# Finding a capacity threshold two bits per step instead of one, in a post-LN mixture-of-experts block on one Trainium2 core

## The chip, the cores and the metric

The program runs on one core of one Trainium2 chip. The metric is device time in microseconds (us) of one execution; the value for a kernel is the median of several executions, and lower is better. A separate execution is recorded by the hardware profiler and gives the profile and the trace that are read below.

## The reference, cut to what matters

The block has two layers, each an attention-like mixer and a mixture of experts, with layer normalisation after each. The change is in the first mixture of experts, where every expert chooses its tokens:

```python
T = B * S                      # 8 * 512 = 4096 tokens
cap = max(1, T // E)           # E = 8 experts, so 512 tokens each
probs = jax.nn.softmax(xt @ Wg, axis=-1)
pT = probs.T                   # 8 x 4096
_, top_idx = jax.lax.top_k(pT, cap)
sel = zeros((E, T), bool).at[arange(E)[:, None], top_idx].set(True)
masked = where(sel, pT, -inf)
assigned = sel.any(axis=0)
tok2exp = where(assigned, argmax(masked, axis=0), argmax(pT, axis=0))
```

So each expert needs its 512 largest probabilities out of 4096. The kernel gets them through a threshold: for each expert, the largest 32-bit pattern t such that at least 512 of its probabilities, read as floats, are at or above t. Probabilities lie between 0 and 1, and for non-negative floats the order of the bit patterns is the order of the values, so t can be found bit by bit from the top, from bit 29 down to bit 0.

## The kernel before, in words

The program has four stages, one after the other: three recurrent layers (`recurrent_layers`), the first mixture of experts (`expert_choice_layer`), attention (`attention_layer`), and the second mixture of experts (`token_choice_layer`). In the profiled execution the recurrent layers end at about 402 us, and the expert stage's first dense matmuls start after 500 us.

Between these lies the routing. `expert_choice_gates` (L1009) computes the softmax over eight experts (L1020 to L1031), transposes it on TensorE into `pt`, copied to SBUF at L1040, in which 16 partitions hold one expert, each with 256 of its tokens, and then searches the threshold in a loop of 30 steps over bits 29 to 0:

- L1055, VectorE: compare all 128 x 256 probabilities with the candidate `cand` and add up the hits of each partition into `cnt` (one instruction with an accumulator output; the profile shows it as two, TENSOR_SCALAR_CACHE_REDUCE and DVE_READ_ACCUMULATOR).
- L1059, TensorE: multiply by the matrix `blk` of ones in 16 x 16 blocks, so that every partition of an expert gets that expert's total `tot`, in PSUM.
- L1061, VectorE: `less` = (tot < 512) times the bit.
- L1063, VectorE: one instruction that clears the bit where there were too few and sets the next bit to be tried.

Each step needs the step before, so the loop is one chain that goes from VectorE to TensorE and back. After it, L1075 to L1114 turn the threshold into the choice `M` of an expert for each token, L1137 to L1160 into places in the experts' lists, and L787 to L820 into a table of tiles. GpSimd then writes the tokens into the lists (L731), SyncE loads the expert weights that the table names (L925), and the expert matmuls follow.

The order within the engines around the loop is set by a scheduler, which fills each engine's queue in program order as far as data and buffers allow; the stages before and the list writing after have their order written out by hand. Two queues matter besides VectorE and TensorE. GpSimd fills a tile `m0none` (memset L723) and writes numbers into it (iota L724). SyncE then issues small loads and stores in this order: L710, L713, L715, then L727, which stores `m0none` and waits for the iota, then L1014, which loads `blk`, and L1016. The first matmul of the search needs `blk`.

Of the kernel before, what the change touches and what calls it, by code (L numbers as in the profile page):

```python
# [10 lines left out]
F32 = mybir.dt.float32  # L11
I32 = mybir.dt.int32
AF = mybir.ActivationFunctionType
ALU = mybir.AluOpType
# [3 lines left out]
P = 128  # L18
# [8 lines left out]
CAP = T // E0  # L27
# [981 lines left out]
def expert_choice_gates(nc, rp, psR, ident, lg, a, M, W):  # L1009


    NS = NC // 2
    blk = rp.tile([P, P], F32, name="blk")
    nc.sync.dma_start(blk, a["c_blk"])  # L1014
    low = rp.tile([P, P], F32, name="low")
    nc.sync.dma_start(low, a["c_low"])  # L1016

    ex = rp.tile([P, NC, E0], F32, name="ex0")
    st = rp.tile([P, NC], F32, name="st0")
    nc.vector.reduce_max(st, lg, AX.X)  # L1020
    nc.vector.tensor_sub(ex, lg, st.unsqueeze(2).to_broadcast([P, NC, E0]))
    nc.scalar.activation(ex, ex, AF.Exp)
    nc.vector.reduce_sum(st, ex, AX.X)
    nc.vector.reciprocal(st, st)
    pr = rp.tile([P, 2, E0, NS], F32, name="pr0")
    for jh in range(2):
        nc.vector.tensor_mul(
            pr[:, jh].rearrange("p e s -> p s e"),
            ex.rearrange("p (s j) e -> p j s e", j=2)[:, jh],
            st.rearrange("p (s j) -> p j s", j=2)[:, jh].unsqueeze(2).to_broadcast([P, NS, E0]),  # L1030
        )  # L1031


    pt_ps = psR.tile([P, 2 * P], F32, tag="x", name="pt_ps")
    for jh in range(2):
        nc.tensor.transpose(
            pt_ps[:, jh * P : (jh + 1) * P], pr[:, jh].rearrange("p e s -> p (e s)"), ident
        )
    pt = rp.tile([P, 2 * P], F32, name="pt")
    nc.vector.tensor_copy(pt, pt_ps)  # L1040

    one = rp.tile([P, 1], F32, name="one")
    nc.vector.memset(one, 1.0)
    desc = rp.tile([P, E0, NS], F32, name="desc")
    for e in range(E0):
        nc.vector.memset(desc[:, e, :], float(E0 - e))

    cand = rp.tile([P, 1], I32, tag="cand", bufs=2, name="cand29")  # L1050
    nc.vector.memset(cand, 1 << 29)
    for bit in range(29, -1, -1):
        hit = rp.tile([P, 2 * P], F32, tag="hit", bufs=2, name=f"hit{bit}")
        cnt = rp.tile([P, 1], F32, tag="cnt", bufs=2, name=f"cnt{bit}")
        nc.vector.tensor_scalar(  # L1055
            hit, pt, cand.bitcast(F32), None, ALU.is_ge, ALU.add, accum_out=cnt
        )
        tot = psR.tile([P, 1], F32, tag="x", name=f"tot{bit}")
        nc.tensor.matmul(tot, blk, cnt, start=True, stop=True)  # L1059
        less = rp.tile([P, 1], I32, tag="less", bufs=2, name=f"less{bit}")  # L1060
        nc.vector.tensor_scalar(less, tot, float(CAP), float(1 << bit), ALU.is_lt, ALU.mult)  # L1061
        new = rp.tile([P, 1], I32, tag="cand", bufs=2, name=f"cand{bit - 1}")
        nc.vector.scalar_tensor_tensor(  # L1063
            new, less, (1 << bit) >> 1, cand, ALU.bitwise_or, ALU.bitwise_xor
        )
        cand = new
    thr = cand

    thr_f = thr.bitcast(F32)
    sel = rp.tile([P, 2 * P], F32, name="sel")  # L1070
    eq = rp.tile([P, 2 * P], F32, name="eq")
    rank = rp.tile([P, 2 * P], F32, name="rank")
    ngt = rp.tile([P, 1], F32, name="ngt")
    left = rp.tile([P, 1], F32, name="left")
    nc.vector.tensor_scalar(sel, pt, thr_f, None, ALU.is_gt, ALU.add, accum_out=ngt)  # L1075

    sl_ps = psR.tile([P, 2, 4 * P], F32, tag="s", bufs=1, name="sl_ps")[:, :, :P]
    S = sl_ps.rearrange("p j (e s) -> p j e s", e=E0)
    for jh in range(2):
        nc.tensor.matmul(  # L1080
            sl_ps[:, jh, :], sel[:, jh * P : (jh + 1) * P], ident, start=True, stop=False
        )
    nc.vector.tensor_scalar(eq, pt, thr_f, None, ALU.is_equal)
    nc.vector.tensor_tensor_scan(
        rank, one.to_broadcast([P, 2 * P]), eq, 0.0, ALU.mult, ALU.add
    )
    before = psR.tile([P, 1], F32, tag="x", name="before")
    nc.tensor.matmul(before, blk, ngt, start=True, stop=False)
    nc.tensor.matmul(before, low, rank[:, 2 * P - 1 : 2 * P], start=False, stop=True)
    nc.vector.tensor_scalar(left, before, -1.0, float(CAP), ALU.mult, ALU.add)  # L1090
    nc.vector.scalar_tensor_tensor(eq, rank, left, eq, ALU.is_le, ALU.mult)
    for jh in range(2):
        nc.tensor.matmul(
            sl_ps[:, jh, :], eq[:, jh * P : (jh + 1) * P], ident, start=False, stop=True
        )


    def across(src, dst):
        nc.vector.tensor_reduce(dst, src.rearrange("p j e s -> p j s e"), AX.X, ALU.max)

    def spread(v):
        return v.unsqueeze(2).to_broadcast([P, 2, E0, NS])

    sl = rp.tile([P, 2, E0, NS], F32, name="sl")
    top = rp.tile([P, 2, NS], F32, tag="top", bufs=2, name="top0")
    across(S, top)
    nc.vector.tensor_sub(sl, spread(top), S)
    nc.vector.scalar_tensor_tensor(pr, sl, -4.0, pr, ALU.mult, ALU.add)
    across(pr, W)
    nc.vector.tensor_tensor(sl, pr, spread(W), ALU.is_equal)  # L1110
    nc.vector.tensor_mul(sl, sl, desc.unsqueeze(1).to_broadcast([P, 2, E0, NS]))
    top = rp.tile([P, 2, NS], F32, tag="top", bufs=2, name="top1")
    across(sl, top)
    nc.vector.tensor_tensor(  # L1114
        M.rearrange("p (s j) e -> p j e s", j=2), sl, spread(top), ALU.is_equal
    )


def expert_choice_layer(tc, pre, x_ext, lg, ident, rows, a):
# [3 lines left out]
    with ExitStack() as ctx:  # L1123
# [6 lines left out]
        nc.vector.memset(keep, 1.0)  # L1130
        nc.vector.memset(keep[:, :, 0:1], 0.0)
        expert_choice_gates(
            nc, rp, psX, ident, lg, a, M, x_ext[:, :, D].rearrange("p (s j) -> p j s", j=2)
        )
# [824 lines left out]
```

## Time and profile before

| what | value |
|---|---|
| median of 7 executions | 1996.2 us (1989.55 to 1999.2) |
| profiled execution, its own time | 1998.94 us |
| span in its trace, first to last instruction | 1997.1 us |
| mean granted TensorE clock over the span | 0.930 |
| TensorE matmul busy | 1737.8 us (87%) |
| VectorE busy | 1132.4 us (57%) |
| ScalarE busy | 1002.3 us (50%) |
| GpSimd busy | 523.1 us (26%) |
| threshold search, first L1055 to first L1075 | 406.32 to 453.04 us: 46.72 us |

In the profile, PE is TensorE (PEld its weight loads), DVE is VectorE, ACT is ScalarE, POOL is GpSimd and SP is SyncE (SPq its queue of transfers). Times on the trace are us from the start of the span. A line of the timeline gives start, duration, engine, source line, operation, output tile and input tiles, the shape, the count, and in brackets how long the engine had been idle and what released it. The float32 matmul of the search appears as two matmul records and two weight loads.

### The profile page before, as it was taken

Reading aid. Unit: us, or ns where it says so; the run is one execution under the profiler, and the core shown is the slowest. Engines: PE = TensorE matmul, PEld = TensorE weight load, DVE = VectorE, ACT = ScalarE, POOL = GpSimd, SP = SyncE. Lnnn points to the kernel's source line nnn. Section 1 sums busy time; section 2 is a strip of 40 time slices with the busy share of each in tenths; the row PEclk is TensorE's granted clock in tenths of the full one; section 3 lists DMA queues with packets and bytes.
Section 4 is the critical chain, followed back from the end, with each engine's and each line's share of the span. In section 5 each row is a group of like instructions: output and inputs, shape, how many; then the busy total and the mean of one; then the engine's idle time right before and its main releaser. Section 6 shows DMA issues by size and latency. Waiting matters only on the chain.

```text
span 1997.1 us, 31137 instructions
## 1 busy us (share of the span) xinstructions
PE 1737.8 (87%) x10398; PEld 1136.3 (57%) x10398; DVE 1132.4 (57%) x2844; ACT 1002.3 (50%) x2166; POOL 523.1 (26%) x447
## 2 busy tenths in 40 slices
PE   6999995531799698898989998987999999999995
PEld 2555553321699584222222222323889999999994
DVE  6999998853122531676777786884534222222226
ACT  5899976500132321457666767655534334333343
POOL 1000000004422221001041423233666644444440
PEclk9999998655899797899999999998999999999998
DMA  9990000004554300000010211122675667566548
GB/s 358 402 386 1 1 0 1 32 7 171 187 176 147 118 1 20 13 17 17 17 58 16 62 32 42 46 76 74 175 203 127 152 159 184 110 145 140 117 103 255
DMA packets 115262, 217.10 MB, mean 109 GB/s; under 512 B 17101, under 2 KB 85919, under 8 KB 108320
## 3 DMA queue, kind: packets, MB, share of 16 engines
q1 hardware_dynamic: 81536, 165.77, 25.1%
q0 software_dynamic: 30560, 46.72, 11.5%
q10 hardware_dynamic: 3008, 2.63, 0.4%
q8 instruction: 84, 1.38, 0.3%
q14 instruction: 74, 0.61, 0.1%
HBM read 244.79 MB, written 100.43 MB: 173 GB/s over the span
## 4 chain that ended last, share of the span: by engine, by line
PE 54%; issue 7%; DVE 6%; DMA 4%; ACT 4%; POOL 4%; SPq 0%; POOLq 0%; another core or an unknown queue 0%; ACTq 0%; DVEq 0%
PE s L1668 13%; PE m1h L956 12%; PE m1o L978 12%; PE po L1704 5%; PE qk L1640 3%; PE bv L1587 2%; DVE nmx L1758 2%; ACT pe L1765 2%; DMA res<-z,m0xg 2%; PE v L1566 1%; PE m1xp L943 1%; POOL res L1205 1%; PE t L1680 1%; POOL m0rows L731 1%; PE tot L1059 1%
## 5 line engine op out<-in xcount | busy, mean ns | idle before, releaser
L1758 DVE TENSOR_REDUCE nmx<-s 128x1 f32<-128x512 f32 x512 | 330.0, 686 | 161.6 <-PE t L1680 103.3
L1765 ACT ACTIVATE pe<-t 128x512 f32<-128x512 f32 x512 | 277.8, 594 | 210.2 <-PE t L1680 198.5
L1668 PE MATMUL s<-kT,qT 32*128 32x512 f32 x1024 | 304.5, 669 | 54.5 <-ACT pe L1765 25.7
L1680 PE MATMUL t<-qA,kT 32*128 32x512 f32 x1024 | 293.2, 649 | 2.5 <-ACT pe L1765 2.0
L1817 POOL DMA_INDIRECT acc<-y,at x143 | 221.6, 1550 | 256.7 <-DVE at L1810 161.5
L1668 PEld LDWEIGHTS s<-kT,qT 32*128 32x128 f32 x1024 | 81.8, 190 | 221.6 <-ACT pe L1765 174.6
L962 ACT ACTIVATE m1hT<-m1h,m1ws 128x128 f32<-128x128 f32 x284 | 103.4, 367 | 155.5 <-PE m1h L956 129.3
L962 ACT ACTIVATE m1hT<-m1h,xT 128x128 f32<-128x128 f32 x288 | 105.4, 368 | 149.5 <-PE m1h L956 133.6
L945 DVE COPY m1xq<-m1xp 128x256 f32<-128x256 f32 x143 | 60.6, 424 | 184.6 <-PE m1xp L943 101.6
L1816 DVE TENSOR_SCALAR y<-m1o,gt 128x256 f32<-128x256 f32 x143 | 69.1, 483 | 168.3 <-PE m1o L978 158.3
L731 POOL DMA_INDIRECT m1rows<-x_ext,slot x128 | 126.8, 990 | 120.8 <-ACT pe L1765 77.7
L956 PE MATMUL m1h<-m1xq,xT 128*128 128x128 f32 x1152 | 142.8, 277 | 4.5 <-DVE m1xq L945 3.2
L956 PEld LDWEIGHTS m1h<-m1xq,xT 128*128 128x128 f32 x1152 | 140.8, 194 | 9.2 <-issue 3.6
L956 PEld LDWEIGHTS m1h<-m1xq,m1ws 128*128 128x128 f32 x1136 | 138.7, 193 | 7.0 <-issue 3.5
L956 PE MATMUL m1h<-m1xq,m1ws 128*128 128x128 f32 x1136 | 140.1, 277 | 2.4 <-DVE m1xq L945 2.3
L1704 PE MATMUL po<-pe,V 128*17 128x512 f32 x1024 | 137.4, 609 | 1.2 <-ACT pe L1765 1.2
L978 PE MATMUL m1o<-xT,m1hT 128*128 128x256 f32 x576 | 137.4, 380 | 0.7 <-issue 0.5
L978 PE MATMUL m1o<-m1ws,m1hT 128*128 128x256 f32 x568 | 134.9, 379 | 0.0
L1734 POOL TENSOR_TENSOR AO<-AO,on 128x256 f32<-128x256 f32 x32 | 23.5, 734 | 353.3 <-DVE on L1729 335.7
L964 ACT ACTIVATE m0hT<-m0h 128x128 f32<-128x128 f32 x156 | 43.0, 277 | 143.7 <-PE m0h L956 116.3
L978 PEld LDWEIGHTS m1o<-xT,m1hT 128*128 128x128 f32 x576 | 103.4, 190 | 12.1 <-ACT m1hT L962 0.7
L978 PEld LDWEIGHTS m1o<-m1ws,m1hT 128*128 128x128 f32 x568 | 102.3, 191 | 10.8
(358 smaller groups left out, 2999.5 us busy)
## 6 DMA issues: line engine op xcount, KB each, us to landing
xT<-in_w_pack SPq DMA_DIRECT2D x72, 1034.0 KB
m1ws<-in_w_pack SPq DMA_DIRECT2D x71, 1034.0 KB
m0ws<-in_w_pack SPq DMA_DIRECT2D x39, 1034.0 KB
m0rows<-zero SPq DMA_DIRECT2D x5, 6360.0 KB
m1xg<-m1rows SPq DMA_DIRECT2D x143, 138.0 KB
acc<-zero SPq DMA_DIRECT2D x2, 4096.0 KB
f<-acc SPq DMA_DIRECT2D x16, 512.0 KB
m0rows<-zero SPq DMA_DIRECT2D x1, 4770.0 KB
```

What stands on the lines that cost most here:

```text
L731: ins = self.nc.gpsimd.indirect_dma_start(out=self.rows[:, :], out_offset=bass.IndirectOffsetOnAxis(ap=place, axis=0), in_=row, in_offset= ...
L945: nc.vector.tensor_copy(xq, ps)
L956: nc.tensor.matmul(ps, w[:, o : o + P], xq[:, dc, :], start=(dc == 0), stop=(dc == DC - 1),)
L962: ins = nc.scalar.activation(hT[:, fc, :], ps, AF.Gelu, bias=w[:, o : o + 1])
L978: nc.tensor.matmul(ps, hT[:, fc, :], w[:, o : o + D], start=(fc == 0), stop=(fc == FC - 1))
L1668: mm = nc.tensor.matmul(ps, qTs[u % NR][r, qc * P : (qc + 1) * P], kTs[u % NR][r, :], start=True, stop=True,)
L1680: mm = nc.tensor.matmul(ps, kTs[v % NR][r, kc * P : (kc + 1) * P], qAs[v][r, :], start=True, stop=True,)
L1704: mm = nc.tensor.matmul(po[h4 * HP : h4 * HP + VW, :], V[:, b * NQ + kc, 4 * g + h4, :], pes.pop((u, kc, h4)), start=(kc == 0), stop=(kc = ...
L1758: ins = nc.vector.tensor_reduce(at, ps, AX.X, ALU.max, negate=True)
L1765: ins = nc.scalar.activation(pe, ps, AF.Exp)
L1816: nc.vector.tensor_scalar_mul(y, ps, gt)
L1817: nc.gpsimd.indirect_dma_start(out=R.acc[t % 2][:, :], out_offset=bass.IndirectOffsetOnAxis(ap=at, axis=0), in_=y, in_offset=None, compute ...
```

## The change

The loop takes 15 steps instead of 30. In each, three candidates are counted: the bits found so far with the next two bits set to 01, 10 and 11. The number of candidates with at least 512 hits, 0 to 3, is the value of the two bits. A table `digit` holds, for each step, the four values 0, 1, 2 and 3 times the step's unit; it is filled by 60 memsets of one column each on GpSimd, which in the program stand ahead of the loop. The vector of four candidates for the next step is made by two VectorE instructions: multiply the count by the unit and add the next step's row of `digit`, then or the result with the bits found so far. The last step makes only the result.

```diff
-    cand = rp.tile([P, 1], I32, tag="cand", bufs=2, name="cand29")
-    nc.vector.memset(cand, 1 << 29)
-    for bit in range(29, -1, -1):
-        hit = rp.tile([P, 2 * P], F32, tag="hit", bufs=2, name=f"hit{bit}")
-        cnt = rp.tile([P, 1], F32, tag="cnt", bufs=2, name=f"cnt{bit}")
-        nc.vector.tensor_scalar(
-            hit, pt, cand.bitcast(F32), None, ALU.is_ge, ALU.add, accum_out=cnt
-        )
-        tot = psR.tile([P, 1], F32, tag="x", name=f"tot{bit}")
+    steps = [1 << bit for bit in range(28, -2, -2)]
+    digit = rp.tile([P, len(steps), 4], F32, name="digit")
+    for i, u in enumerate(steps):
+        for j in range(4):
+            nc.gpsimd.memset(digit[:, i, j : j + 1], float(j * u))
+    cand = rp.tile([P, 4], I32, tag="cand", bufs=2, name="cand0")
+    nc.vector.tensor_copy(cand, digit[:, 0, :])
+    for i, u in enumerate(steps):
+        cnt = rp.tile([P, 3], F32, tag="cnt", bufs=2, name=f"cnt{i}")
+        for j in range(3):
+            hit = rp.tile([P, 2 * P], F32, tag="hit", bufs=2, name=f"hit{i}_{j}")
+            nc.vector.tensor_scalar(
+                hit, pt, cand.bitcast(F32)[:, j + 1 : j + 2], None, ALU.is_ge, ALU.add,
+                accum_out=cnt[:, j : j + 1],
+            )
+        tot = psR.tile([P, 3], F32, tag="x", name=f"tot{i}")
         nc.tensor.matmul(tot, blk, cnt, start=True, stop=True)
-        less = rp.tile([P, 1], I32, tag="less", bufs=2, name=f"less{bit}")
-        nc.vector.tensor_scalar(less, tot, float(CAP), float(1 << bit), ALU.is_lt, ALU.mult)
-        new = rp.tile([P, 1], I32, tag="cand", bufs=2, name=f"cand{bit - 1}")
-        nc.vector.scalar_tensor_tensor(
-            new, less, (1 << bit) >> 1, cand, ALU.bitwise_or, ALU.bitwise_xor
-        )
+        k = rp.tile([P, 1], F32, tag="digits", bufs=2, name=f"k{i}")
+        reach = rp.tile([P, 3], F32, tag="reach", bufs=2, name=f"reach{i}")
+        nc.vector.tensor_scalar(reach, tot, float(CAP), None, ALU.is_ge, ALU.add, accum_out=k)
+        more = rp.tile([P, 4], I32, tag="more", bufs=2, name=f"more{i}")
+        new = rp.tile([P, 4], I32, tag="cand", bufs=2, name=f"cand{i + 1}")
+        if i + 1 < len(steps):
+            nc.vector.scalar_tensor_tensor(
+                more, k.to_broadcast([P, 4]), float(u), digit[:, i + 1, :], ALU.mult, ALU.add
+            )
+        else:
+            nc.vector.tensor_scalar_mul(more, k.to_broadcast([P, 4]), float(u))
+        nc.vector.tensor_tensor(new, more, cand[:, 0:1].to_broadcast([P, 4]), ALU.bitwise_or)
         cand = new
+    cand = cand[:, 0:1]
     thr = cand
```

In the built program of the changed kernel, the order of all other instructions on each engine is as before. The 60 memsets stand in GpSimd's queue between the memset L723 and the iota L724; the copy that makes the first candidates stands in VectorE's queue where the memset L1051 stood, ahead of the reciprocal L1024.

## Prediction

> **What bounds the kernel now.** The page's shares over the whole span do not settle this change: TensorE is busy 87% of the time, but the search sits in a stretch where nearly everything else is idle. So I read the chain of work that ended last, cut to the search (406.3 to 453.1 us):
>
> ```profile
> by line: PE tot L1059 38.4%; DVE hit L1055 32.0%; DVE less L1061 10.9%; DVE cand L1063 10.6%; issue 7.7%; DVE sel L1075 1.0%; DVE cand-1_2589 L1063 0.4%
> ```
>
> The whole stretch is one chain through the four instructions of the loop; the table of the same stretch has ScalarE and GpSimd at 0.00 us, transfers at a share of 0.00, and a granted TensorE clock of 0.50. Nothing hides the loop, and it hides nothing. One step, from the timeline (PE weight-load line left out):
>
> ```profile
> 409.49 0.48 DVE L1055 TENSOR_SCALAR_CACHE_REDUCE hit<-pt,cand 128x256 f32<-128x256 f32 x1
> 409.89 0.08 DVE L1055 DVE_READ_ACCUMULATOR hit<-pt,cand 128x1 f32 x1
> ...
> 410.03 0.58 PE L1059 MATMUL tot<-cnt,blk 128*128 128x1 f32 x2 [0.97 <-DVE hit L1055]
> 410.65 0.16 DVE L1061 TENSOR_SCALAR less<-tot 128x1 int32<-128x1 f32 x1 [0.68 <-PE tot L1059]
> 410.85 0.16 DVE L1063 SCALAR_TENSOR_TENSOR cand<-less,cand 128x1 int32<-128x1 int32 x1
> 411.04 0.48 DVE L1055 TENSOR_SCALAR_CACHE_REDUCE hit<-pt,cand 128x256 f32<-128x256 f32 x1
> ```
>
> A step is 411.04 - 409.49 = 1.55 us: 1.16 from the start of the count to the start of `less` (count, trip to TensorE and back), 0.20 for `less`, 0.19 for `cand`. An instruction that waits for its forerunner on VectorE starts 0.04 us after that one's end. Thirty steps take 406.32 to 453.04, 46.72 us.
>
> **What the change removes, adds and moves.** VectorE's main instructions stay at 90 (30 x 3 before, 15 x 6 after). What goes is 15 trips to TensorE; what comes is that three counts stand side by side without data between them, and that the last three instructions of a step are a little longer.
>
> *The three counts.* The first and second need only the candidates. The third reuses the first one's `hit` buffer (two buffers) and so waits for the first count, which ends 0.48 us after its start. How closely counts follow each other when nothing holds them, no row shows for this very form; these come nearest, the start of an instruction behind an accumulating one with no wait in between:
>
> ```profile
> 380.15 0.42 DVE L394 SCALAR_TENSOR_TENSOR junk<-Y 128x256 f32<-128x256 f32 x1
> ...
> 380.50 0.42 DVE L394 SCALAR_TENSOR_TENSOR junk<-Y 128x256 f32<-128x256 f32 x1
> ```
> ```profile
> 453.04 0.48 DVE L1075 TENSOR_SCALAR_CACHE_REDUCE sel<-pt,cand-1_2589 128x256 f32<-128x256 f32 x1
> ...
> 453.45 0.35 DVE L1083 TENSOR_SCALAR eq<-pt,cand-1_2589 128x256 f32<-128x256 f32 x1
> ```
>
> L1075 is the same operation on the same tile as the count, and its follower starts 0.41 us after it, before its 0.48 us are over; L394's follows after 0.35. I take 0.41. The low end is 0.35; the high end is 0.48 + 0.04 = 0.52, each count waiting for the one before to end. The third count's wait is over at about 0.52, before its turn at 0.82, so I cost it at nothing; at the high end it is included. Two extra counts: 2 x 0.41 = 0.82 us a step.
>
> The Trainium skill ("VectorE: DVE Perf Modes", section "The DRAIN you can't avoid") says that the next op does not start until the pipe has emptied, that eight copies took the same time with a semaphore after each or after the last only, and (section "Rules for kernel authors") that one should "Minimize op *count*, not sems". By that the counts would stand at the waiting spacing and most of the gain would go, since the op count is the same. The same page allows an earlier start to an op that is not held, and the two rows above, where the follower starts inside the other's duration, side with that; the rule keeps a chance as the first rival.
>
> *The trip.* TensorE moves 3 columns in place of 1. L865 moves 8 columns in 0.56 us at the same clock of 0.50, against 0.58 here, so: no change, 1.16 us from the last count's start to `reach`. The matmul pairs come at longer intervals; the clock is at the lowest value in the windows, 0.50, from 407 to 500 us already, whatever the density, so I cost this at nothing.
>
> *`reach`, `more`, new candidates.* `reach` is a compare with an accumulator over 3 columns from PSUM. The nearest row is L795, the same operation over 8 columns, with a follower that waits for it:
>
> ```profile
> 468.66 0.22 DVE L795 TENSOR_SCALAR_CACHE_REDUCE lem<-cumm,m0pnw 128x8 f32<-128x8 f32 x1
> ...
> 468.92 0.22 DVE L798 TENSOR_SCALAR_CACHE_REDUCE lem<-cumm,m0pno 128x8 f32<-128x8 f32 x1
> ```
>
> From start to start 0.26. From below it is `less`, 0.20 with no accumulator. `more` waits for two engines, VectorE (`reach`) and GpSimd (`digit`, long filled), and the program has a separate wait instruction in front of it. L1157 is the nearest such case, waiting for L1149 on VectorE and for TensorE, long done:
>
> ```profile
> 464.53 0.42 DVE L1149 TENSOR_TENSOR cnt<-upto,tot 128x256 f32<-128x256 f32 x1
> 465.05 0.36 DVE L1157 TENSOR_TENSOR pl<-rk,cnt 128x128 f32<-128x128 f32 x1
> ```
>
> It starts 0.10 us after the other's end where 0.04 is usual: 0.06 more, in 14 of 15 steps (bounds: 0 and 0.12). So `reach` 0.26 + 0.06. `more` and the new candidates are 128x4; L1063's 0.16 us and 0.20 or 0.19 to the next start hold for 128x1, and 128x8 rows such as L830 take 0.17, so 0.20 + 0.19.
>
> *Sum of a step:* 0.82 + 1.16 + 0.32 + 0.20 + 0.19 = 2.69 us. Fifteen: 40.35, less 0.06 in the last step, 40.29. Against 46.72: **6.43 us saved**.
>
> *Ahead of the loop.* The first candidates are now a copy, in place of a 0.06 us memset; the small cast L862 takes 0.14, so I add 0.1 (bounds 0 and 0.2). It waits for the first four memsets only, which come two microseconds earlier. The 60 memsets on GpSimd push back the iota L724, and behind it in SyncE's queue the store L727 and the load of `blk` L1014, which the first matmul needs:
>
> ```profile
> 0.26 0.10 POOL L1947 MEMSET const-float32-0.0<- 128x1 f32 x1 [0.26 <-issue]
> ...
> 0.34 0.12 POOL L1947 MEMSET const-uint8-127<- 128x1 uint8 x1
> ...
> 401.87 0.33 POOL L723 MEMSET m0none<- 128x276 f32 x1 [393.47 <-ACT table L680]
> 402.27 0.13 POOL L724 IOTA m0none<- 128x2 int32 x1
> ```
> ```profile
> 403.17 0.43 SPq L727 DMA_DIRECT2D m0rows<-m0none  x1
> 403.64 0.43 SPq L1014 DMA_DIRECT2D blk<-in_c_blk  x1
> ```
>
> Four one-column memsets start within 0.08 us, 0.03 apart. At that pace 60 take 1.8 us: the iota ends at 402.20 + 1.8 + 0.13 = 404.1, L727 goes at about 404.2, L1014 0.47 later, and lands some 1.97 us after that (the chain has L727's store landing 1.97 after its start; an estimate for `blk`), at 406.6. The first matmul now comes after three counts, at 406.86 + 0.82 = 407.7. So cost nothing, covered by the counts. In general `blk` is late by 60p - 2.8 us, where p is the time per memset. Low end 0; at p = 0.10, each memset's full duration, 3.2 us.
>
> *After the loop* nothing but its result starts work: GpSimd waited 64.2 us for L1157, SyncE's next transfer is L925 at 471 us, behind the table, and GB/s is near 0 in the slices of the search. What the loop saves, everything behind it starts earlier by, and the instruction order behind it is unchanged.
>
> **The sum.** 6.43 - 0.1 = 6.3 us. The profiled execution's 1998.94 us (span 1997.1, 1.8 around it) would become 1992.6. It ran 2.7 us above the median of the seven, 1996.2; I take the saving off the median: **1989.9 us**.
>
> **The rivals.**
>
> 1. *The counts do not overlap* (spacing 0.52). 30 x 0.11 = 3.3 us come back: 3.0 saved, 1993.2 us. Against it, the two rows above; for it, that no row shows this form behind itself without a wait. The rule of the Trainium skill quoted above would give this case. 15%.
> 2. *`blk` comes late by some.* p = 0.10: 3.2 us come back, 1993.1 us. Against it, the four memsets 0.03 apart. 8%.
> 3. *Slower: GpSimd's memsets run one at a time with a start-up each.* L1863, a small copy alone on GpSimd, takes 0.24 us; at p = 0.24 `blk` is late by 11.6 us, 5.3 more than is saved: 2001.5 us. It decides from p = 0.15 on (60 x 0.15 - 2.8 = 6.2). Against it, the same rows; L749, a lone one-column memset, takes 0.10. 5%.
> 4. *The saving does not arrive*: something after 453 us waits for what the loop does not set. About 1996 us. No such wait is in the rows after the loop. 6%.
>
> My forecast, with the spacing between 0.35 and 0.46, keeps 66%.
>
> **How the numbers follow.** 0.2% is 4 us, about what a measurement of this kernel can tell from no change. The forecast saves 6.3; with spacing 0.35 (1.8 more) and no cost for the double wait (0.8 more) it is 1987.3, and scatter of the medians takes the low end to 1986. The high end is rivals 1 and 2 at 1993 with some 3 us for scatter (the seven runs spread over 9.6 us): 1996. Rival 3 and part of rival 4 lie outside. Faster by over 0.2%: the forecast and a little of 1 and 2, 0.68. Within: 1, 2 and 4, 0.26. Slower: 0.06.
>
> **What would show it.** In the profile after: 15 steps 2.69 us apart, and the loop from first count to L1089 (the old L1075) 40 us; the second and third count 0.41 behind the one before; `reach` 1.16 after the last count's start; `more` 0.32 after `reach`; the iota before 405 us and the first matmul right behind the third count. If the steps are 2.9 or more, rival 1 holds; if the first matmul stands idle after its counts with a transfer as its releaser, 2 or 3. If the loop is 40 us and the total is not lower, rival 4. What would make it wrong altogether is a TensorE trip that grows with three columns, or a `reach` much over 0.3.

## The result, and the profile after

| | before | changed kernel |
|---|---|---|
| median, same chip | 1995.93 us (47 runs, 1987.2 to 2001.19) | 1988.54 us (19 runs, 1980.26 to 1994.26) |
| ratio, 95% interval | | 0.9962 [0.9952, 0.9972], so -7.6 us [-9.6, -5.6] |
| profiled execution / its span | 1998.94 / 1997.1 us | 1983.48 / 1981.7 us |
| mean granted TensorE clock | 0.930 | 0.933 |
| threshold search, first count to `sel` | 46.72 us | 39.51 us |

Two repeats of the changed kernel, each beside runs of the kernel before on its own chip, gave 0.9963 [0.9951, 0.9975] and 0.9964 [0.9949, 0.9979].

The two profiled executions differ by 15.4 us, twice what the medians do. Only 7.2 us of it is in the search (46.72 - 39.51). The search begins 1.9 us earlier (406.32 against 404.39, behind code that the change does not touch), and from `sel` to the end it is 1544.1 against 1537.8 us. Those two parts are scatter between executions, as the repeats below show. So I read the window of the search by itself and not the span.

The table of that window for the kernel before and, below it, for the changed kernel; its columns are the window and its length, busy time and (in brackets) records of PE, PEld, DVE, ACT and POOL, then the granted clock, the share of the transfers and GB/s:

```profile
406.32:453.04 46.72, 17.57 (x60) 15.03 (x60) 24.15 (x120) 0.00 (x0) 0.00 (x0) 0.50 0.00 1
404.39:443.90 39.51, 8.76 (x30) 7.49 (x30) 26.72 (x150) 0.00 (x0) 0.00 (x0) 0.50 0.01 2
```

Half the TensorE records are left (30 for 60), VectorE has 30 records more (60 accumulator reads for 30, beside 90 main instructions in both), everything else is still idle, and the clock is still 0.50. In the trace of this execution the chain that ended last breaks off near its end, so the chain of the search is read from the second repeat (search 406.51 to 446.03 us); it answers to the chain shown of before:

```profile
by line: DVE hit L1061 49.2%; PE tot L1066 22.7%; issue 7.3%; DVE reach L1069 6.8%; DVE cand L1078 6.5%; DVE more L1073 6.1%; DVE sel L1089 1.2%; DVEq L1073 0.7%; DVE more L1077 0.5%
```

It is still one chain, through VectorE and TensorE by turns, but TensorE's share has gone from 38.4% to 22.7% and the counts' from 32.0% to 49.2%. One step of the changed kernel, from the timeline:

```profile
409.72 0.48 DVE L1061 TENSOR_SCALAR_CACHE_REDUCE hit<-pt,cand 128x256 f32<-128x256 f32 x1
...
410.12 0.47 DVE L1061 TENSOR_SCALAR_CACHE_REDUCE hit<-pt,cand 128x256 f32<-128x256 f32 x1
...
410.52 0.47 DVE L1061 TENSOR_SCALAR_CACHE_REDUCE hit<-pt,cand 128x256 f32<-128x256 f32 x1
...
411.06 0.58 PE L1066 MATMUL tot<-cnt,blk 128*128 128x3 f32 x2 [2.05 <-DVE hit L1061]
...
411.69 0.16 DVE L1069 TENSOR_SCALAR_CACHE_REDUCE reach<-tot 128x3 f32<-128x3 f32 x1 [0.68 <-PE tot L1066]
411.77 0.08 DVE L1069 DVE_READ_ACCUMULATOR reach<-tot 128x1 f32 x1
411.96 0.16 DVE L1073 SCALAR_TENSOR_TENSOR more<-k,digit 128x4 int32<-128x4 f32 x1
412.16 0.16 DVE L1078 TENSOR_TENSOR cand<-more,cand 128x4 int32<-128x4 int32 x1
```

The second and third count start 0.40 us behind the one before, inside its 0.48 us. `reach` starts 1.17 us after the third count, `more` 0.27 after `reach`, the candidates 0.20 after `more`, and the next count 0.20 after them (at 412.36, not shown). Over all fifteen the step is 2.63 us (39.51 / 15).

The head of the search in the same timeline (SPq is SyncE's queue):

```profile
400.19 2.04 POOL L1054 MEMSET digit<- 128x1 f32 x60
...
402.10 0.15 DVE L1056 CAST cand<-digit 128x4 int32<-128x4 f32 x1
...
402.18 0.13 POOL L724 IOTA m0none<- 128x2 int32 x1
...
402.34 0.34 SPq L727 DMA_DIRECT2D m0rows<-m0none  x1
...
402.73 0.43 SPq L1014 DMA_DIRECT2D blk<-in_c_blk  x1
...
405.73 0.59 PE L1066 MATMUL tot<-cnt,blk 128*128 128x3 f32 x2 [1.84 <-DVE hit L1061]
```

The 60 memsets take 2.04 us, 0.034 each; the transfer of `blk` is issued at 402.73; and the first matmul's releaser is the third count, not the transfer.

### The profile page after: what moved, and what is told of

Its sections match the earlier page's. It is cut to its first block, busy times and chain, and to the rows that moved or that the text cites. A ratio compares the mean times of both kernels' runs of the same rounds, so it can differ in the third digit from the quotient of the medians.

```text
span 1981.7 us, 31181 instructions
## 1 busy us (share of the span) xinstructions
PE 1721.9 (87%) x10368; PEld 1123.2 (57%) x10368; DVE 1129.4 (57%) x2874; ACT 1003.4 (51%) x2166; POOL 525.8 (27%) x507
## 3 DMA queue, kind: packets, MB, share of 16 engines
q0 software_dynamic: 30560, 46.72, 11.7%
q10 hardware_dynamic: 3008, 2.63, 0.4%
## 5 line engine op out<-in xcount | busy, mean ns | idle before, releaser
L956 PE MATMUL m1h<-m1xq,xT 128*128 128x128 f32 x1152 | 143.5, 278 | 4.8 <-issue 3.1
L956 PEld LDWEIGHTS m1h<-m1xq,xT 128*128 128x128 f32 x1152 | 141.4, 194 | 9.4 <-issue 3.9
L956 PEld LDWEIGHTS m1h<-m1xq,m1ws 128*128 128x128 f32 x1136 | 137.4, 192 | 6.6 <-issue 3.2
L956 PE MATMUL m1h<-m1xq,m1ws 128*128 128x128 f32 x1136 | 138.7, 275 | 2.0 <-DVE m1xq L945 1.9
```

Source lines behind the costliest of these rows:

```text
L956: nc.tensor.matmul(ps, w[:, o : o + P], xq[:, dc, :], start=(dc == 0), stop=(dc == DC - 1),)
```

## The experiments

The theory to be tested: the change gains what 15 trips to TensorE and back cost, less 30 extra counts at the unheld spacing of VectorE, and nothing else moves. The rivals of the prediction are tested with it: counts that do not overlap (rival 1), `blk` late (rivals 2 and 3), a saving that does not reach the end (rival 4). Absolute times differ from chip to chip, so each total is given against the kernel before on the same chip.

### One buffer for the hits: what the overlap is worth

```diff
-            hit = rp.tile([P, 2 * P], F32, tag="hit", bufs=2, name=f"hit{i}_{j}")
+            hit = rp.tile([P, 2 * P], F32, tag="hit", bufs=1, name=f"hit{i}_{j}")
```

With one buffer each count has to wait for the one before to end: the same instructions, with a wait more.

> The changed kernel with one hit buffer in place of two, so that each count waits for the end of the one before. Theory (the counts gain by overlapping): the second and third count start 0.52 us after the one before in place of 0.40, a step takes 2.64 + 0.24 = 2.88 us, the search 43.1 us against 39.5, and the total is 3.6 us above the changed kernel's. Rival (a wait between counts is free, the gain has another source): spacing, search and total unchanged, 39.5 us.

One step's counts in its timeline:

```profile
412.67 0.48 DVE L1061 TENSOR_SCALAR_CACHE_REDUCE hit<-pt,cand 128x256 f32<-128x256 f32 x1
413.08 0.08 DVE L1061 DVE_READ_ACCUMULATOR hit<-pt,cand 128x1 f32 x1
413.20 0.48 DVE L1061 TENSOR_SCALAR_CACHE_REDUCE hit<-pt,cand 128x256 f32<-128x256 f32 x1
413.60 0.08 DVE L1061 DVE_READ_ACCUMULATOR hit<-pt,cand 128x1 f32 x1
413.72 0.48 DVE L1061 TENSOR_SCALAR_CACHE_REDUCE hit<-pt,cand 128x256 f32<-128x256 f32 x1
```

Counts 0.52 or 0.53 us apart, each 0.04 after the end of the accumulator read of the one before; the search takes 43.25 us (406.85 to 450.10). So this is rival 1 made on purpose, and its price is 3.7 us (43.25 - 39.51), half the gain. The total was 0.999 [0.9978, 1.0002] of the kernel before; the changed kernel was not run on that chip, so the 3.7 us are read from the search alone. That the change has its whole gain hangs on two buffers for a tile that nobody reads.

### Four times the memsets, first try: another wait

```diff
-        for j in range(4):
-            nc.gpsimd.memset(digit[:, i, j : j + 1], float(j * u))
+        for j in range(16):
+            nc.gpsimd.memset(digit[:, i, j % 4 : j % 4 + 1], float(j % 4 * u))
```

> The changed kernel with every memset of the digit table issued four times, 240 in place of 60. Theory (blk is late by what the memsets push it back beyond the cover of the first three counts): at the measured 0.034 us each the memsets take 8.2 us, the iota moves back by 6.1 us to 408.3 on the changed kernel's time line, the load of blk is issued at 408.9 and lands near 410.8, and the first matmul starts there instead of at 405.73: 5 us later, the total 5 us above the changed kernel's. Rival (the load is covered anyway, or the memsets hide): first matmul and total unchanged.

180 of the memsets came behind the iota, as the timeline shows:

```profile
402.90 2.04 POOL L1054 MEMSET digit<- 128x1 f32 x60
...
404.89 0.13 POOL L724 IOTA m0none<- 128x2 int32 x1
404.97 5.99 POOL L1054 MEMSET digit<- 128x1 f32 x180
...
405.44 0.43 SPq L1014 DMA_DIRECT2D blk<-in_c_blk  x1
...
409.15 0.22 DVE L1056 CAST cand<-digit 128x4 int32<-128x4 f32 x1 [4.26 <-POOL digit L1054]
```

`blk` was on time. Instead the cast that makes the first candidates waited 4.26 us for GpSimd's repeats, with the softmax behind it in VectorE's queue: the search started 4.25 us later behind L723 (8.72 us after it, 4.47 in the changed kernel) and took its 39.5 us. The total was 0.9998 [0.9986, 1.0009]. A miss as a test of rivals 2 and 3. It shows that the cast binds VectorE's queue to GpSimd's last write into the four columns that the cast reads. It does not wait for all of `digit`: it starts at 409.15, and the repeats run on to 410.96 (404.97 + 5.99). If they went through the table in three rounds of 60, which the trace does not name, the third round began an estimated 4.0 us behind 404.97 (two thirds of 5.99), and these columns were last written at about 409.1. The prediction had this wait right for the changed kernel, as one for the first four memsets; writing the columns again moves it back.

### The memsets in front of the iota: `blk` made late

```diff
+    pad = rp.tile([P, 180], F32, name="pad")
+    for j in range(180):
+        nc.gpsimd.memset(pad[:, j : j + 1], 0.0)
     cand = rp.tile([P, 4], I32, tag="cand", bufs=2, name="cand0")
```

The added memsets fill a tile that nobody reads, so the cast is free of them.

> The changed kernel with 180 more one-column memsets on GpSimd, into a tile of their own that nothing reads, ahead of the iota, so that the store behind the iota and the load of blk are issued later while the candidates are there in time. Theory (blk is covered by the first three counts only up to 60p = 2.8 us): 240 memsets take 8.1 us, the iota moves back by 6.1 us, the load of blk is issued about 408.8 on the changed kernel's time line and lands 2.0 to 2.7 later, the first matmul starts 5 to 5.7 us later than at 405.73, with the load as its releaser; the later steps are unchanged at 2.64, and the total is 5 to 6 us above the changed kernel beside it. Rival (the store in between or the load costs less than I think, or the matmul does not wait for it): first matmul right behind the third count, total unchanged.

```profile
401.06 2.04 POOL L1054 MEMSET digit<- 128x1 f32 x60
...
403.03 5.99 POOL L1057 MEMSET pad<- 128x1 f32 x180
...
406.08 0.47 DVE L1064 TENSOR_SCALAR_CACHE_REDUCE hit<-pt,cand 128x256 f32<-128x256 f32 x1
...
408.98 0.13 POOL L724 IOTA m0none<- 128x2 int32 x1
...
409.52 0.43 SPq L1014 DMA_DIRECT2D blk<-in_c_blk  x1
...
411.77 0.56 PE L1069 MATMUL tot<-cnt,blk 128*128 128x3 f32 x2 [7.00 <-DMA blk<-in_c_blk]
```

Now the iota comes at 408.98, `blk` is issued at 409.52, and the first matmul starts 2.25 us after that, with the transfer as its releaser. Without the delay it would have started at 406.61 (the first count at 405.27, plus 1.34 as in the changed kernel), so it is 5.2 us late. The prediction's formula, 60p - 2.8, gives the same with the 7.96 us that the 240 memsets took (401.06 to 409.02) in place of 60p: 7.96 - 2.8 = 5.2. That it fits so closely is in part luck, since two of its terms were off in opposite directions: from the end of the memsets to the issue of `blk` it is 0.50 us where the prediction had 0.67, and from the issue to the landing 2.12 by the chain of this trace where it had 1.97. The search grows to 44.65 us, and the total to 0.9996 [0.9981, 1.0011], where the changed kernel on the same chip had 0.9964; by the medians that is 8.2 us above the changed kernel, where 5 to 6 were expected. Rivals 2 and 3 were real mechanisms with a formula that fits; what decided was the pace of the memsets. With 2.25 us from issue to matmul, `blk` would have been ready at 404.98 in the changed kernel, an estimated 0.75 us before it was needed. That time is not the same in every run: in the kernel below with one count on ScalarE the first matmul starts 2.74 us after the issue of `blk` (405.88 to 408.62) and the trace names the transfer as its releaser, and with 2.74 us the cover in the changed kernel would be an estimated 0.26 us. By the formula `blk` is late from 0.047 us per memset on (2.8 / 60).

### Ten idle steps appended: does a microsecond of search arrive at the end

```diff
+    for i in range(10):
...
+        nc.vector.tensor_scalar(less, tot, -1.0, 1.0, ALU.is_lt, ALU.mult)
...
+        nc.vector.scalar_tensor_tensor(new, less, 0, cand, ALU.bitwise_or, ALU.bitwise_xor)
+        cand = new
```

Ten steps of the kernel before, with a bound that no count is below, so that the candidate stays as it is.

> The changed kernel with ten more steps of the one-bit form behind its search, which leave the threshold as it is. Theory (search time goes into the total one for one, nothing behind it is set by anything else): ten times 1.556, 15.6 us more in the search and in the total, 2004.1 us where the changed kernel has 1988.5 and before 1995.9, a ratio to before of 1.0041. Rival (part of the search's time is covered by something else, or the later stages run faster because the search ends earlier): the total moves by clearly less or more than 15.6 us.

The search took 55.04 us, 15.5 more than in the changed kernel (ten steps of 1.55), 8.3 more than in the kernel before. The total was 1.0056 [1.0037, 1.0074], that is +11.1 us [+7.3, +14.7] against the kernel before. The 8.3 us arrive, and perhaps some more; a search that cost nothing at the end (rival 4) would have left the total where it was.

### Three bits at a time on VectorE alone

```diff
-    steps = [1 << bit for bit in range(28, -2, -2)]
+    steps = [1 << bit for bit in range(27, -3, -3)]
...
-        for j in range(3):
+        for j in range(7):
```

and tiles of 7 and 8 columns instead of 3 and 4.

> The search by three bits at a time: ten steps with seven counts each, otherwise as the changed kernel. Theory (a step is 0.40 for each count beyond the first, 1.16 for the last count and the trip, 0.67 for the rest): 6 x 0.40 + 1.16 + 0.67 = 4.23 us a step, 42.3 us for the search, 2.8 above the changed kernel's 39.5 and 4.4 below the 46.7 of before. Rival 1 (what counts is the number of trips to TensorE and back, counts are cheap): below 39.5 us. Rival 2 (counts cost 0.52 when more of them follow each other): 49.5 us, slower than before.

The search took 42.55 us, 4.25 a step, with 0.25 us of error in the whole search: ten steps with 7 counts lose to fifteen with 3. The step model holds (0.40 for each extra count, 1.16 for the last count and the trip, 0.67 behind, 0.39 in the one-bit form): 30 steps of 1.55 us, 15 of 2.63, 10 of 4.25, and two bits is the best of the three. The total missed: 1.0001 [0.9989, 1.0013], where -4.2 us were due. So it was run once more:

> Three bits a step on VectorE alone, again. Its search took 42.55 us, as expected, but its total came out 0.2 us above before (interval -2.2 to +2.6) where 4.2 below was due. Theory (search time arrives in the total one for one, the miss was scatter): 3.0 us above the changed kernel beside it, ratio to before 0.998. Rival (something behind the search takes back what this form saves): again level with before, 7 us above the changed kernel.

Again 42.55 us of search, and 0.9983 [0.9966, 0.9999], -3.4 us; by the medians it is 4.1 us above the changed kernel on that chip, nearer to the 3.0 of the theory than to the rival's 7. The miss of the first total was not the search.

### The double wait

In the last step `more` needs no row of `digit`, and so waits for VectorE only:

```profile
443.39 0.08 DVE L1069 DVE_READ_ACCUMULATOR reach<-tot 128x1 f32 x1
443.50 0.17 DVE L1077 TENSOR_SCALAR more<-k 128x4 int32<-128x4 f32 x1
```

It starts 0.03 us behind the end of its forerunner, where the step shown above has 0.11 (411.85 to 411.96). To take the second wait out of the other steps, the digits of the next step are or-ed with the bits found so far while TensorE multiplies, so that `more` is a plain product:

```diff
+        pre = rp.tile([P, 4], I32, tag="pre", bufs=2, name=f"pre{i}")
+        nc.vector.tensor_tensor(pre, digit[:, i + 1, :], base, ALU.bitwise_or)
...
-            nc.vector.scalar_tensor_tensor(
-                more, k.to_broadcast([P, 4]), float(u), digit[:, i + 1, :], ALU.mult, ALU.add
-            )
...
+        nc.vector.tensor_scalar_mul(more, k, float(u))
```

The table holds integers in this kernel, and `more` has one column in place of four.

> The changed kernel with the or of the found bits and the next step's digits done while TensorE counts, so that the instruction behind the accumulator waits for VectorE alone. Theory (the double wait costs 0.08 us a step: 0.105 between the end of reach and more, against 0.03 in the last step, where there is no double wait): the gap falls to 0.03, a step takes 2.55 us, the search 38.3 us, 1.2 less than the changed kernel's. Rival (the gap belongs to the accumulator output, not to the double wait): the gap stays at 0.1 and the search at 39.5 us.

```profile
412.97 0.16 DVE L1070 TENSOR_TENSOR pre<-digit,cand 128x4 int32<-128x4 int32 x1
...
413.82 0.08 DVE L1074 DVE_READ_ACCUMULATOR reach<-tot 128x1 f32 x1
413.94 0.15 DVE L1077 TENSOR_SCALAR more<-k 128x1 int32<-128x1 f32 x1
```

The gap is 0.03 or 0.04 in every step, the search 38.44 us: 1.07 less, 0.08 in each of 14 steps, for one VectorE instruction a step more, which is hidden. The form of `more` changed with its waits, but the form does not explain the gap: in the kernel before, L1063 has the same operation, SCALAR_TENSOR_TENSOR, with one wait, and starts 0.04 us behind its forerunner (410.81 to 410.85). In the changed kernel's trace 14 separate wait instructions of VectorE's queue stand at L1073, and none at `more` here. That is the price of the double wait. The total, 0.9964 [0.9951, 0.9977] beside the changed kernel's 0.9963 on the same chip, is too coarse for 1 us.

### A share of the counts for ScalarE

ScalarE is idle during the search. In the next kernel it makes one of the three counts as a sum of signs, on top of the edit before. VectorE's two counts are turned round with it, to hits below the candidate, and `cand` and `cnt` get 16 buffers in place of 2 (neither is in the cut):

```diff
+        nc.scalar.activation(
+            sgn, pt, AF.Sign, bias=cand.bitcast(F32)[:, 1:2], scale=-1.0,
+            accum_out=cnt[:, 0:1],
+        )
-        for j in range(3):
+        for j in range(1, 3):
...
-        nc.vector.tensor_scalar(reach, tot, float(CAP), None, ALU.is_ge, ALU.add, accum_out=k)
+        nc.vector.scalar_tensor_tensor(reach, tot, 1.0, most, ALU.mult, ALU.is_le, accum_out=k)
```

A sum of signs counts a probability equal to the candidate as half a hit. The bound in `most` is set so that one such tie changes nothing; two or more in one expert could.

> As the run before, with one of the three counts of a step on ScalarE, as a sum of signs of candidate minus probability (the bound for it is 3073 in place of at most 3584 below; two probabilities of one expert that equal a candidate exactly would be counted as one). Theory (a step is bound by the counts on VectorE, 0.40 each beyond the first): ScalarE's count ends about 0.7 us after the candidates, before VectorE's two at 0.88; a step takes 2.55 - 0.40 + 0.06 for the second engine that TensorE waits for, 2.2 to 2.3 us, the search 33 to 34.5 us, and the total is 12 us below before. Rival (the engines hold each other up, or ScalarE is the later one): the search stays at 38 us or more.

The search took 33.35 us, 5.1 less than with all three counts on VectorE (38.44). The trip is 1.22 or 1.23 us here where it was 1.16 or 1.17 (1.28 in the first step, whose matmul the trace puts down to `blk`); whether the second engine in front of the matmul adds the 0.06 is not separated from `pre`, which the trace names as the releaser of most of these matmuls. The total was 0.9944 [0.9923, 0.9964]. With seven counts, four on VectorE and three on ScalarE, three bits at a time:

> Three bits a step, ten steps, four counts on VectorE and three on ScalarE. Theory: VectorE's four counts take 3 x 0.40 + 0.48 = 1.69 us, ScalarE's three about 0.1 + 2 x 0.37 + 0.57 = 1.4 us and are covered; a step is 3 x 0.40 + 1.22 + 0.66 = 3.1 us, the search 31 us, and the total is 15 us below before. Rival (ScalarE's accumulators keep its counts apart, 0.6 each): ScalarE ends at 1.9 us and sets the step, 3.3 us, the search 33 us, no better than the run before.

```profile
413.59 0.48 DVE L1070 TENSOR_SCALAR_CACHE_REDUCE hit<-pt,cand 128x256 f32<-128x256 f32 x1
413.65 0.51 ACT L1064 ACTIVATE sgn<-pt,cand 128x256 f32<-128x256 f32 x1 [1.45 <-DVE cand L1089]
...
414.07 0.19 ACT L1064 ACTIVATION_READ_ACCUMULATOR sgn<-pt,cand 128x1 f32 x1
414.16 0.50 ACT L1064 ACTIVATE sgn<-pt,cand 128x256 f32<-128x256 f32 x1
...
414.65 0.50 ACT L1064 ACTIVATE sgn<-pt,cand 128x256 f32<-128x256 f32 x1
...
415.05 0.19 ACT L1064 ACTIVATION_READ_ACCUMULATOR sgn<-pt,cand 128x1 f32 x1
415.20 0.09 DVE L1070 DVE_READ_ACCUMULATOR hit<-pt,cand 128x1 f32 x1
...
415.43 0.57 PE L1075 MATMUL tot<-cnt,blk 128*128 128x7 f32 x2 [2.47 <-DVE pre L1079]
```

ScalarE's counts follow each other at 0.49 to 0.51 us, not at the 0.37 that I had expected, and its third one ends at 415.24, just before VectorE's fourth at 415.29. The two engines are nearly balanced, and VectorE still sets the step: the chain of work in it runs through VectorE's counts and has no piece of ScalarE. The search took 30.31 us, 3.03 a step. So with ScalarE's help the optimum moves from two bits to three, and the search is 16.4 us below the kernel before. The total was 0.9931 [0.9912, 0.9951]; it was run once more beside the changed kernel:

> Three bits a step with four counts on VectorE and three on ScalarE, again, for its total: search 30.3 us, 9.2 less than the changed kernel beside it, and 16.4 below before, a ratio of 0.992. Rival (part of it is given back behind the search, as the total of 13.8 below before in its first run could mean): 12 us below before or less, 4 to 5 below the changed kernel.

30.30 us, and 0.9938 [0.9914, 0.9961], where the changed kernel had 0.9964 on that chip. The interval against the kernel before still holds the 16.4 us that the theory had, but both medians come out near the rival's: 12.4 us below before and 4.3 below the changed kernel, where the theory had 16.4 and 9.2. This version beats both kernels: by 13.8 and 12.4 us against the one before, and its medians are 6.0 and 4.3 us below the changed kernel's on the same chips (1980.9 against 1986.85, 1983.85 against 1988.1).

### The changed kernel again, and where the time goes behind the search

The changed kernel ran in both later groups, for comparison:

> The changed kernel again, beside the runs that follow. In the first four runs the total against before lay 1.5 to 4.4 us above what the change of the search and of the lead to it accounts for. Theory (that is scatter): search 39.5 us, total 7.2 us below before, a ratio of 0.9964. Rival (a few us are given back behind the search): search 39.5 us, total only 4 to 5 us below before, a ratio of 0.9977.

> The changed kernel once more, as the reference for the three runs that follow on the same chip. Both theories: search 39.5 us, total 7 to 8 us below before.

Its search took 39.52 us both times: across executions and chips the search repeats to 0.01 us. All totals beside what the search and the lead in front of it (from L723 to the first count, 4.45 us before) make due:

| kernel | search us | due us | measured us [95%] |
|---|---|---|---|
| changed kernel | 39.51 | -7.2 | -7.6 [-9.6, -5.6] |
| changed kernel, first and second repeat | 39.52 | -7.2 | -7.4 [-9.8, -5.0]; -7.2 [-10.2, -4.2] |
| one buffer for the hits | 43.25 | -3.5 | -2.0 [-4.4, +0.4] |
| four times the memsets (lead +4.27) | 39.5 | -2.9 | -0.4 [-2.8, +1.8] |
| `blk` late | 44.65 | -2.0 | -0.8 [-3.8, +2.2] |
| ten idle steps | 55.04 | +8.3 | +11.1 [+7.3, +14.7] |
| three bits, VectorE alone, first and second run | 42.55 | -4.2 | +0.2 [-2.2, +2.6]; -3.4 [-6.8, -0.2] |
| no double wait | 38.44 | -8.2 | -7.2 [-9.8, -4.6] |
| one count on ScalarE | 33.35 | -13.4 | -11.2 [-15.3, -7.2] |
| three on ScalarE, three bits, first and second run | 30.31 | -16.4 | -13.8 [-17.5, -9.8]; -12.4 [-17.1, -7.8] |

The due value lies in the interval in eleven of thirteen runs; in the first run with three bits and, by under 0.2 us, in the one with the repeated memsets the whole interval lies above it. The traces say how far the saving can be followed. From the start of `sel` to the group of expert matmuls (L956) from which on the groups start at the same distances in all six traces (3.5, 3.1, 3.1, 4.6, then 3.7 us), the kernel before takes 81.15 us, the changed one 81.71, 81.25 and 81.43, the two runs with three bits on two engines 80.03 and 81.41. The last matmul into `m0h` (L956) starts 209.1 us behind `sel` before, 209.6, 209.1 and 209.4 in the changed kernel, 207.9 and 209.3 with three bits on two engines. So what the search saved is still there when these matmuls end, 209 us later, within 1.2 us. From the even groups to the end the same code took 1462.9 us before, 1456.1, 1456.3 and 1453.4 in the changed kernel, 1461.3 and 1463.7 with three bits on two engines, a spread of 10 us, which the totals carry too. The largest part of it lies between the last matmul into `m0h` and the first attention scores (tile `s`): 113.4 us before, 105.4, 110.3 and 105.5 in the changed kernel, 110.8 and 113.2 with three bits on two engines. What makes that stretch longer or shorter is not shown. What stays open is a remainder: the ten totals of the other kernels lie 0.8 to 4.4 us above what is due and none below. Those of one group share their runs of the kernel before, so they are not ten independent witnesses, but that some variants lose a few us late in the program is not excluded. The two runs with three bits on two engines point that way most: against the changed kernel on the same chips they were 5 and 10 us longer in the late part, in one profiled execution each, and their medians fell 3.3 and 5.0 us short of the 9.2 us that the search saves over it.

## Why the prediction was right, point by point

1989.9 us stood against 1988.54 measured, and 6.3 us of saving against 7.6 [5.6, 9.6]; the search itself saved 7.2.

- **What bounds the loop.** Right: one chain, nothing beside it. The 7.2 us that the changed kernel's search saved arrived, by the totals of three groups (7.6, 7.4 and 7.2).
- **Spacing of the counts, 0.41.** Measured 0.40. The row of the same operation with an unheld follower was the right one to go by. The run with one buffer shows the other end of the range, 0.52, and what it would have cost: 43.25 - 39.51 = 3.7 us, where I had put 3.3 on rival 1: half of the gain, not most of it as the prediction's paragraph on the Trainium skill says. The Trainium skill says in "VectorE: DVE Perf Modes", section "Rules for kernel authors", that one should reduce the number of operations, not of semaphores, and in "The DRAIN you can't avoid" that in the eight copies measured there a semaphore costs nothing extra. This case disagrees for these operations: the two kernels have the same operations in the search, and 0.12 us goes with each added wait between counts. The same section's remark that an operation that is not held starts earlier is the part that the trace bears out, 0.40 against a duration of 0.48.
- **The trip, 1.16.** Right: 1.16 or 1.17 from the last count's start to `reach` in fourteen steps, 1.22 in one, and in the two runs with three bits on VectorE alone 1.16 to 1.24 with seven columns. The clock stayed at 0.50, as costed.
- **`reach` 0.26 + 0.06 for the double wait.** Measured 0.27 or 0.28 for both, as 0.20 + 0.08. Without the double wait `more` follows `reach` after 0.20 (413.74 to 413.94 in that kernel), less than the 0.26 that L795 has over 8 columns: of my two ends, the lower one, `less`, was the nearer. The double wait cost 0.08 where I had 0.06, so the two errors partly cancel.
- **`more` and the candidates, 0.20 + 0.19.** Right: 0.20 and 0.20, or 0.19, from step to step.
- **Sum of a step, 2.69.** 2.63 measured; the difference is 2 x 0.01 in the counts and 0.04 in `reach` and its wait. Over the fifteen steps this is the 0.8 us by which the search was shorter than the 40.29 forecast.
- **The copy, 0.1.** Nothing: from L723 to the first count it is 4.45 us before and 4.47 after. The cast runs at 402.10 between the end of the reduction in front of it and a small memset, and the reciprocal behind it starts 0.09 us after it.
- **`blk` covered, at 0.03 a memset.** Right, and 0.034 measured. But the cover was thinner than I wrote: I had `blk` 1.1 us ahead of the first matmul, and by the run with `blk` late it was an estimated 0.75, by the kernel with one count on ScalarE 0.26.
- **The rivals.** 1 did not happen, and needs one buffer less to happen. 2 and 3 did not, by the pace of the memsets, and their formula held when `blk` was made late. 4 is excluded for the greater part by the ten idle steps and by the 209 us behind the search. The three-column trip and a long `reach`, named as what would make the forecast wrong, stayed small.

## What to carry to other kernels

A loop that is one chain between two engines pays for its round trips: take the step apart into the part per trip (here 1.16 + 0.67 us, the last count included) and the part per piece of work (0.40 us), and the best number of pieces per trip followed here with an error of under one per cent on VectorE alone (42.3 us expected, 42.55 measured); when an idle engine takes a share, the optimum moves. Work put side by side on one engine only overlaps if nothing makes it wait, and that includes the buffers of results that nobody reads. Where setup work is moved to an idle engine, follow the queue behind it to what the loop first needs, and the instruction that reads its result: here both were harmless by less than a microsecond or by a scheduler's order.

## What the runs showed of the hardware

- Unheld counts of 128x256 with an accumulator start 0.40 us apart on VectorE, 0.52 with a wait between. ScalarE's counts of the same size stand 0.49 to 0.51 apart with no wait between them. In the step shown, the first one's accumulator read (414.07, 0.19 long) starts 0.09 before the count ends, and the next count (414.16) 0.10 before the read ends: each overlaps the one before it, and the read adds 0.09. The Trainium skill ("ScalarE: Activation LUTs", section "What ACT_TABLE_LOAD costs") states 280 ns and 0.833 ns an element for such an operation, and an overlap of some 93 ns with the next; by that the spacing would be an estimated 0.40. The trace agrees with the duration (0.49 by the page, 0.50 here), and by these records the accumulator read, which the page does not count, is the difference.
- From the issue of the load of `blk` on SyncE's queue to the start of the matmul that waited for it were 2.25 us in one run and 2.74 in another (landed, by the chains, after 2.12 and 2.60).
- One-column memsets on GpSimd follow each other at 0.033 to 0.034 us, though each lasts 0.10: 240 of them took 7.96 us.
- An instruction of VectorE that waits for two engines started 0.08 us later than one that waits for one, even where the second had long been done. In the chain shown above it is DVEq L1073, VectorE's queue, at 0.7% of 39.5 us, or 0.02 us each time: the record accounts for a quarter of the price, and the rest is idle time around it.
